# Moving products of the first chunk's feed-forward layer in between its last adapters

## Chip, cores and metric

The kernel runs on one core of one Trainium2 chip. The metric is the device time of one execution in microseconds (us); lower is better. All data are float32.

## The reference, cut to what matters

`x` holds 32 batches of 64 rows (tokens here) by 1024 columns. Four residual layers follow each other:

```python
x = x + ssm_convolution(x)                      # FFT convolution, masked by length
x = x + einsum('bsi,boi->bso', x, W1[id1])      # one 1024x1024 weight per batch
x = x + einsum('bij,bkj->bik', x, W2[id2])      # another one per batch
gate = x @ W_gate.T + 0.5 * (x @ A_gate[id].T) @ B_gate[id].T    # 2752 hidden rows
up   = x @ W_up.T   + 0.5 * (x @ A_up[id].T)   @ B_up[id].T
act  = silu(gate) * up
x = x + act @ W_down.T + 0.5 * (act @ A_down[id].T) @ B_down[id].T
```

The two middle layers are called adapters below: each batch picks one of 16 weights for each of them. The last layer is the gated feed-forward layer with a low-rank term of rank 16 per batch.

## The kernel before, in words

The 32 batches are cut in four chunks of eight, so a chunk has 512 token columns (`TC`); x lies with its 1024 features on 128 partitions in eight k tiles. The convolution of all chunks comes first. Then the 16 adapters of chunk 0 run (eight batches, two layers; batch b's second layer comes after batch b+1's first). Then `ffn` (L902) runs for each chunk, and the adapters of the next chunk are slipped into its matmuls.

An adapter (L297) takes eight weight tiles of 512 KB, each in 16 matmuls' worth of records on TensorE (PE); then VectorE (DVE) transposes the result and adds it to x. Weight tiles come over SyncE's (SP's) DMA queue into `wpool`, nine rotating buffers (`ROTATING`). Some tiles of the first adapters were fetched during the convolution into memory of their own (`early`, `late`), which is used up before the twelfth adapter.

In the gated layer 2688 of the 2752 hidden rows are computed by a Strassen-Winograd scheme with seven products for eight: in chunk 0 on halves of the tokens (256 columns, `TH`) and of the features (`halves`, L526), later on quarters (`quarters`, L624). The last 192 rows, the plain ones, are `rest` (L781), ordinary products with three weight tiles `wr`. The scheme needs sums of weights (`stationary`, `sides`, L481 to L488) and sums of x (`moving`, L495; `moving_of`, L848), all on DVE. In chunk 0 `halves` also makes the sums of a second level for the later chunks: `kept` (L534) writes a block of sums into one of two buffers, and a DMA on GpSimd's (POOL's) queue stores it (L548). A third and a fourth block of the same call (L603, L608) wait for the stores of the first two.

A call of `halves` has two column blocks m = 0, 1, and in each the products 0, 5, 6, 4, 1, 2, 3 in that order, four matmuls of 256 columns each. Product 1 adds onto product 0's bank, 2 onto that of 5 and 4, 3 onto that of 6; DVE adds and ScalarE (ACT) copies the results out between them. `gated` (L745) makes two calls, gate and up. After the first pair of blocks `ffn` runs `rest` and then the down products (L1063), whose terms for the plain rows need `rest1`.

The low-rank products (`low_rank`, L420) multiply x by columns of 32 for each pair of batches: four pairs, each into its own 32 partitions of one bank.

PE's order is that of the program throughout (manual schedule, L129). DVE's and ACT's is so from L349 on, that is once the memory of the first phase is given back (`first.close()`, L347); the other queues are ordered by the framework's scheduler. Between the adapters stand, before the change, only products of the first plain weight tile: the first 256 tokens behind the twelfth adapter (`LEFT_AT`), and then, behind the last one, the next 128 (L331).

Of the kernel before, what the change touches and what calls it, by code (L numbers as in the profile page):

```python
# [19 lines left out]
P = 128  # L20
# [12 lines left out]
MG = 2  # L33
NG = FM // MG
EARLY = 16
LEFT_AT = 11
LATE = 7
FIRST_LOADS = 8
MORE_LOADS = 3
# [37 lines left out]
def kernel(  # L77
# [38 lines left out]
    def ps_tile(name):  # L116
        return psum.tile([P, 512], F32, tag="ps", name=name)
# [200 lines left out]
    def adapters(c):  # L318
        for layer, b in layers(c):
            yield adapter(layer, b)  # L320

    def left_tile():
        wt = wpool.tile([P, KT, P], F32, tag="w", name="wr0_0")
        nc.sync.dma_start(wt.rearrange("p k f -> p (k f)"), wr[0])
        return wt, ps_tile("pr0_0")

    def left_part(wt, ps, t0, t1):

        tokens = slice(t0, t1)
        for kt in range(KT):  # L330
            nc.tensor.matmul(  # L331
                ps[:, tokens],
                wt[:, kt, :],
                xs[0][:, kt, tokens],
                start=(kt == 0),
                stop=(kt == KT - 1),
            )


    for i, _ in enumerate(adapters(0)):  # L340
        if i == LEFT_AT:
            left0 = left_tile()
            left_part(*left0, 0, TH)

    left_part(*left0, TH, TH + TQ)
    done_first = [loads[-1]]
    first.close()  # L347

    ctx.enter_context(tc.manual_schedule(engines={DVE, ACT}))  # L349
# [67 lines left out]
    def pair(j):  # L417
        return slice(2 * R * j, 2 * R * (j + 1))

    def low_rank(at, n, x_of, name):  # L420


        ps = ps_tile(f"pl_{name}")[:, : 2 * H]
        for i in range(n):
            x_i = x_of(i)
            for j in range(BC // 2):
                nc.tensor.matmul(  # L427
                    ps[pair(j)],
                    at[:, i, pair(j)],
                    x_i[:, 2 * H * j : 2 * H * (j + 1)],  # L430
                    start=(i == 0),
                    stop=(i == n - 1),
                )
        return ps
# [72 lines left out]
    def low_rank_of(c, gi, g):  # L507
        name = f"{c}_{gi}_{g}"
        lt, copy = expand(b_rows(c, 2 * gi + g), name, [("gu"[g], i) for i in range(4)])
        return lt.rearrange("p (i m) t -> p i m t", i=2), copy  # L510

    def halves_sides(gi, g, m):

        name = f"{gi}_{g}_{m}"
        wt = []
        for i in (0, 1):
            pool, tag, bufs = (wpool, "w", ROTATING) if i or m else (gpool, "wx", 1)
            t = pool.tile([P, 2, KH, P], F32, tag=tag, name=f"wf{i}_{name}", bufs=bufs)
            nc.sync.dma_start(
                t.rearrange("p k s f -> p (k s f)"), (wg, wu)[g][i, MG * gi + m]  # L520
            )
            wt.append(t)
        st = qpool[0].tile([P, 3, KH, P], F32, tag=f"s{m}", name=f"s_{name}")
        return wt, st, stationary(wt, KH, st)

    def halves(c, gi, g, o, xb, sides0, early, also=lambda: None):  # L526

        name = f"{c}_{gi}_{g}"
        lt, copy_lt = low_rank_of(c, gi, g)
        wts, sts, sides_of = ([x] for x in sides0)  # L530

        kept_first = []
# [35 lines left out]
        for m in range(MG):  # L568
            ws = sides_of[m]

            def product(ps, j, start):
                for kt in range(KH):
                    nc.tensor.matmul(  # L573
                        ps,
                        ws[j][:, kt, :],
                        xb[j][:, kt, :],
                        start=start and kt == 0,
                        stop=kt == KH - 1,
                        skip_group_check=True,
                    )  # L580


            pa, pb, pc = (ps_tile(f"pf{i}_{name}_{m}")[:, :TH] for i in range(3))
            c11, c12, c21, c22 = (
                o[:, i, m, t * TH : (t + 1) * TH] for i in (0, 1) for t in (0, 1)
            )
            u, v = (
                gpool.tile([P, 2 * TQ], F32, tag=f"u{i}", name=f"u{i}_{name}_{m}", bufs=1)
                for i in range(2)
            )  # L590
            product(pa, 0, True)
            nc.scalar.copy(u, pa)
            product(pb, 5, True)
            nc.scalar.copy(v, pb)
            nc.vector.tensor_add(u, v, u)
            if m == 0:
                copy_lt()
                for at_, x in zip((wts, sts, sides_of), halves_sides(gi, g, 1)):
                    at_.append(x)
                also()  # L600
            else:
                kept_parts()
                kept(2)  # L603
            product(pc, 6, True)
            nc.vector.tensor_add(c22, pc, u)
            product(pb, 4, True)
            nc.vector.tensor_add(c22, pb, c22)  # L607
            kept(3 * m)  # L608
            product(pa, 1, False)
            nc.scalar.copy(c11, pa)  # L610
            product(pb, 2, False)
            nc.vector.tensor_add(c12, pb, u)
            if m == 0:
                kept(1)
            else:
                early()
            product(pc, 3, False)
            nc.vector.tensor_add(c21, pc, u)
            o_m = o[:, :, m]
            nc.vector.tensor_add(o_m, o_m, lt[:, :, m])  # L620
# [3 lines left out]
    def quarters(c, gi, g, o, xb, _, early, also=lambda: None):  # L624
# [117 lines left out]
        (p3,) = unit((2,), lambda: None)  # L742
        add(c12, c12, p3)

    def gated(c, gi, xb, sides0, between, early):  # L745

        f = quarters if c else halves
        act = apool.tile([P, 2, MG, TC], F32, tag="act", name=f"act_{c}_{gi}")  # L750
        sides0 = f(c, gi, 0, act, xb, sides0, lambda: fill(1.3 if c else 2.6))
        between(2 * gi)

# [27 lines left out]
    def rest(c):  # L781


        wts, pss = [], []

        def load():
            i = len(wts)
            wt = wpool.tile([P, KT, P], F32, tag="w", name=f"wr{i}_{c}")
            into = wt.rearrange("p k f -> p (k f)")
            last_wr[:] = [nc.sync.dma_start(into, wr[i]).ins]  # L790
            wts.append(wt)

        def products():
            i = len(pss)
            ps = ps_tile(f"pr{i}_{c}")
            for kt in range(KT):
                nc.tensor.matmul(  # L797
                    ps,
                    wts[i][:, kt, :],
                    xs[c][:, kt, :],  # L800
                    start=(kt == 0),
                    stop=(kt == KT - 1),
                )
            pss.append(ps)

        if c == 0:
            left_part(*left0, TH + TQ, TC)
            wts.append(left0[0])
            pss.append(left0[1])
            nc.scalar.copy(rest1, pss[0])  # L810
            yield
        else:
            load()
        bt = b_rows(c, 2 * NG)
        load()
        yield
        if c:
            products()
            nc.scalar.copy(rest1, pss[0])
        yield  # L820
        products()
        lt, copy = expand(bt, f"{c}_rest", (("g", 0), ("u", 1), ("u", 2), ("g", 2)))
        copy()
        nc.vector.tensor_add(lt[:, 0], lt[:, 0], rest1)
        nc.vector.tensor_add(lt[:, 1], pss[1], lt[:, 1])
        nc.scalar.activation(rest1, lt[:, 0], AF.Silu)
        nc.vector.tensor_mul(rest1, rest1, lt[:, 1])
        load()
        products()
        v, up = lt[:, 2], lt[:, 3]  # L830
        nc.vector.tensor_add(v, pss[2], v)
        nc.scalar.copy(up[SECOND], v[FIRST])
        a = rest2.rearrange("p i t -> p (i t)")
        nc.gpsimd.memset(a[FIRST], 0.0)
        nc.scalar.activation(a[SECOND], v[SECOND], AF.Silu)
        nc.vector.tensor_mul(a[SECOND], a[SECOND], up[SECOND])
        yield
# [7 lines left out]
        ps = low_rank(at, KT, lambda i: x_c[:, i, :], f"{name}_{c}")  # L845
        nc.vector.tensor_mul(tms[name], ps, bmask)

    def moving_of(c):  # L848

        x_c = xs[c]  # L850
        xq = [
            x_c[:, k * KH : (k + 1) * KH, t * TH : (t + 1) * TH]
            for k in (0, 1)
            for t in (0, 1)
        ]

        if c == 0:
            xd = qpool[0].tile([P, 7, KH, TH], F32, tag="xd", name=f"xd_{c}")
            for i, q in enumerate((0, 2, 3)):
                nc.scalar.copy(xd[:, 4 + i], xq[q])  # L860
            xb = moving(*xq, *(xd[:, i] for i in range(4)))
            return (xd[:, 4], xd[:, 5], xd[:, 6], *xb[3:])


        xd = qpool[0].tile([P, 7, 7, KQ, TQ], F32, tag="xd", name=f"xd_{c}")

# [251 lines left out]
        return steps[0] if more_come else None  # L1118

    tables = [columns(ag, 0, KT, "g_0"), columns(au, 0, KT, "u_0", ("cu", "lt"))]  # L1120
    ats = [in_order() for in_order in tables]
    xb = moving_of(0)
    for name, at in zip("gu", ats):
        prepare(0, name, at)
    sides0 = halves_sides(0, 0, 0)
    for c in range(NCK):
        xb = ffn(c, xb, sides0, adapters(c + 1) if c + 1 < NCK else iter(()))
        sides0 = None
# [490 lines left out]
```

## Time and profile before

| what | value |
|---|---|
| median of 3 runs (lowest, highest) | 2311.53 us (2307.45, 2314.43) |
| profiled execution, its span | 2313.8 us |
| PE busy, share | 2249.8 us, 97% |
| PE weight loads | 1868.0 us, 81% |
| DVE | 1320.6 us, 57% |
| ACT | 380.0 us, 16% |
| POOL | 270.6 us, 12% |
| mean granted PE clock | 0.998 |
| DMA | 684.96 MB, 296 GB/s |
| twelfth adapter of chunk 0 ends | 286.87 us |
| sixteenth adapter of chunk 0 ends | 329.83 us |
| first product of the first gated call | 338.68 us |
| second gated call's first product | 364.40 us |
| first product of the later `rest` | 393.13 us |
| down products begin | 408.17 us |

The profile is one execution, 2.3 us longer than the median. Times in it count from its first instruction. A matmul in float32 shows as two records, and the shown end of the last record of a group lies a little behind the start of the next group, because matmuls are pipelined; the pace is read from starts. L numbers are lines of the kernel before. In a timeline row the brackets give how long the engine was idle before the row and what it waited for.

### The profile page before, as it was taken

To read this page: it belongs to the slowest core of one execution; us is meant where nothing else is said; L and a number is where in the kernel's file an instruction comes from. 1 tells how busy PE (TensorE), PEld (TensorE's weight loads), DVE (VectorE), ACT (ScalarE), POOL (GpSimd) and SP (SyncE) were. 2 spreads that over 40 slices of the span, in tenths; PEclk is the share of its full clock that TensorE was granted. 3 is DMA by queue.
4 is the path that set the end of the run, shared out by engine and by line. 5 is a ranking of instruction groups with operands and counts; after the bars stand their busy time and mean duration, and the time that the engine had idled before them with its cause. 6 is when DMAs were issued, how large, how long until landed. Compare 5 with 4: busy or idle time off the path is not lost.

```text
span 2313.8 us, 53743 instructions
## 1 busy us (share of the span) xinstructions
PE 2249.8 (97%) x21706; PEld 1868.0 (81%) x21706; DVE 1320.6 (57%) x2791; ACT 380.0 (16%) x822; POOL 270.6 (12%) x388
## 2 busy tenths in 40 slices
PE   5999989999999999999999999999999999999999
PEld 4996557787777789688778889688769889799998
DVE  7511127567446776546535676646535676477585
ACT  4300001011001112111102212121102212121220
POOL 3423003111101121000000011000000011100000
PEclk9999999999999999999999999999999999999999
DMA  8999997879997957879997957879997947285582
GB/s 306 354 370 394 407 403 280 317 289 354 365 343 293 350 174 258 304 285 360 350 357 279 358 167 265 297 292 358 355 351 288 363 152 276 87 298 203 191 280 68
DMA packets 201802, 684.96 MB, mean 296 GB/s; under 512 B 26178, under 2 KB 28482, under 8 KB 201042
## 3 DMA queue, kind: packets, MB, share of 16 engines
q1 hardware_dynamic: 169714, 590.77, 69.5%
q0 software_dynamic: 25184, 82.37, 9.6%
q10 hardware_dynamic: 6656, 8.39, 1.0%
q8 instruction: 171, 2.80, 0.5%
q14 instruction: 77, 0.63, 0.1%
HBM read 614.02 MB, written 67.40 MB: 295 GB/s over the span
## 4 chain that ended last, share of the span: by engine, by line
PE 78%; DMA 14%; issue 5%; DVE 2%; POOL 1%; POOLq 0%; SPq 0%; ACT 0%; DVEq 0%
PE pq L664 28%; PE po L1063 22%; PE pa L304 11%; DMA wa<-in_w 7%; PE pc L1404 5%; PE pf L573 5%; PE pr L797 3%; DMA wa<-sums 2%; DMA sums<-kept 1%; PE pe L456 1%; DMA hk<-kp 1%; PE pl_d L427 1%; DMA kp<-ks 1%; DMA wf<-in_wg 0%; DMA wr<-in_wr 0%
## 5 line engine op out<-in xcount | busy, mean ns | idle before, releaser
L304 PE MATMUL pa<-wa,x 128*32 128x256 f32 x7760 | 449.1, 381 | 19.3 <-DMA wa<-in_w 16.8
L664 PE MATMUL pq<-xd,wa 128*128 128x128 f32 x3360 | 415.9, 275 | 1.3 <-DMA wa<-sums 0.9
L304 PEld LDWEIGHTS pa<-wa,x 128*32 128x32 f32 x7760 | 241.8, 110 | 209.9 <-DMA wa<-in_w 49.1
L664 PEld LDWEIGHTS pq<-xd,wa 128*128 128x128 f32 x3360 | 395.0, 192 | 2.3 <-DMA wa<-sums 2.2
L664 PE MATMUL pq<-xd,wb 128*128 128x128 f32 x2520 | 324.1, 276 | 0.6 <-DVE x L316 0.4
L664 PEld LDWEIGHTS pq<-xd,wb 128*128 128x128 f32 x2520 | 300.7, 192 | 4.7 <-DVE x L316 0.6
L314 DVE STREAM_TRANSPOSE y<-pa 128x512 f32<-128x512 f32 x64 | 45.9, 717 | 286.6 <-PE pa L304 286.6
L1063 PE MATMUL po<-act,wd 128*128 128x256 f32 x640 | 168.6, 386 | 0.0
L1404 PE MATMUL pc<-uf,hk 128*128 128x256 f32 (+7 forms) x1024 | 153.3, 312 | 12.2 <-DMA hk<-kp 9.5
L1063 PE MATMUL po<-actd,s 128*128 128x256 f32 x640 | 164.2, 379 | 0.0
L1063 PE MATMUL po<-actd,wd 128*128 128x256 f32 x640 | 164.2, 379 | 0.0
L1404 PEld LDWEIGHTS pc<-uf,hk 128*128 128x128 f32 x1024 | 148.4, 195 | 16.6 <-issue 7.9
L355 POOL DMA_INDIRECT bgu<-in_bgu,rows x44 | 51.4, 1168 | 924.0 <-PE pe L456 827.2
L573 PE MATMUL pf<-xd,wf 128*128 128x256 f32 x640 | 150.9, 381 | 0.0
L1063 PEld LDWEIGHTS po<-act,wd 128*128 128x128 f32 x640 | 117.8, 190 | 29.9 <-issue 14.6
L482 DVE TENSOR_TENSOR s<-wd 128x256 f32<-128x256 f32 x80 | 33.8, 423 | 184.1 <-PE po L1063 184.0
L573 PEld LDWEIGHTS pf<-xd,wf 128*128 128x128 f32 x640 | 121.2, 191 | 17.4
L1063 PEld LDWEIGHTS po<-actd,s 128*128 128x128 f32 x640 | 121.6, 190 | 16.5
L1063 PEld LDWEIGHTS po<-actd,wd 128*128 128x128 f32 x640 | 121.6, 190 | 16.5
L1095 ACT COPY uo<-po 128x256 f32<-128x256 f32 x48 | 17.9, 373 | 622.3 <-PE po L1063 620.2
L573 PE MATMUL pf<-xd,s 128*128 128x256 f32 x480 | 115.9, 385 | 3.9 <-DVE up L607 2.7
L573 PEld LDWEIGHTS pf<-xd,s 128*128 128x128 f32 x480 | 91.0, 191 | 20.0 <-DVE up L607 4.4
(235 smaller groups left out, 2566.4 us busy)
## 6 DMA issues: line engine op xcount, KB each, us to landing
wa<-in_w SPq DMA_DIRECT2D x485, 512.0 KB, 7.0
wa<-sums SPq DMA_DIRECT2D x210, 512.0 KB, 5.8
wb<-parts SPq DMA_DIRECT2D x120, 384.0 KB, 5.3
wd<-in_wd SPq DMA_DIRECT2D x80, 512.0 KB, 7.0
wb<-in_wq SPq DMA_DIRECT2D x90, 384.0 KB, 5.9
hk<-kp SPq DMA_DIRECT2D x30, 1024.0 KB, 8.8
sums<-kept POOLq DMA_DIRECT2D x30, 1024.0 KB, 7.2
wf<-in_wg SPq DMA_DIRECT2D x20, 512.0 KB, 7.1
```

The costliest lines, as they stand in the source:

```text
L304: nc.tensor.matmul(acc[i * S : (i + 1) * S, s * 256 : (s + 1) * 256], xs[c][:, kt, lo + s * S : lo + (s + 1) * S], wt[:, i * 256 : (i + 1) ...
L314: nc.vector.transpose(y, acc)
L355: nc.gpsimd.indirect_dma_start(out=t, out_offset=None, in_=table, in_offset=bass.IndirectOffsetOnAxis(ap=at_, axis=0),)
L427: nc.tensor.matmul(ps[pair(j)], at[:, i, pair(j)], x_i[:, 2 * H * j : 2 * H * (j + 1)], start=(i == 0), stop=(i == n - 1),)
L456: nc.tensor.matmul(ps[:, at_ * 2 * H : (at_ + 1) * 2 * H], bt[pair(j), g], tms[table][pair(j)], start=(g == 0), stop=True, skip_group_chec ...
L482: nc.vector.tensor_add(s1, a21, a22)
L573: nc.tensor.matmul(ps, ws[j][:, kt, :], xb[j][:, kt, :], start=start and kt == 0, stop=kt == KH - 1, skip_group_check=True,)
L664: nc.tensor.matmul(ps[:, to * TQ : (to + 1) * TQ], w[i][:, k, :], xb[:, j, SLOT[i], k, :], start=start and k == 0 and to == 0, stop=k == K ...
L797: nc.tensor.matmul(ps, wts[i][:, kt, :], xs[c][:, kt, :], start=(kt == 0), stop=(kt == KT - 1),)
L1063: nc.tensor.matmul(pss[j], *term, start=(s0 == m0 and i == 0 and home[j] % 2 == 0), stop=(end and i == len(terms) - 1 and not late), skip_ ...
L1095: nc.scalar.copy(u1, p1)
L1404: nc.tensor.matmul(ps[:, j, d * B :], hk[:, j, d * P : (d + 1) * P], uf[:, i + j, : KT - d, :].rearrange("p k b -> p (k b)"), start=(d == ...
```

## The change

- The memory of the first phase is given back behind the twelfth adapter instead of the sixteenth (`OWN_ENDS`), so that buffers of the gated layer exist from there on; DVE's and ACT's program order begins there too.
- Between the last adapters now stand: the first 256 tokens of all three plain weight tiles (`begin_rest`; only the first tile is kept, the other two are loaded again for the second half in `rest`), products 0 and 1 of both column blocks of the first gated call (`begin_products`), and the low-rank products of gate and up for batch pairs 0 and 1 (`begin_low_rank`). Those of pairs 2 and 3 stay behind the last adapter.
- The four weight tiles of the first gated call are loaded into places of their own (`weight_places`: one buffer of before and the memory of activation tiles that are not in use yet), not into `wpool`: two ahead of the thirteenth adapter, two behind the last one.
- x's sums are made by batches (`part`): batches 4 and 5, then 6, then 7, each as soon as x has them.
- `halves` leaves out products 0 and 1 where they were begun and takes their stored results; `rest` computes only tokens 256 to 511 in chunk 0, and its sums come in two instructions each.

The core of the diff:

```diff
-LEFT_AT = 11
+OWN_ENDS = 12
...
-    for i, _ in enumerate(adapters(0)):
-        if i == LEFT_AT:
-            left0 = left_tile()
-            left_part(*left0, 0, TH)
-
-    left_part(*left0, TH, TH + TQ)
-    done_first = [loads[-1]]
+    layers0 = adapters(0)
+    for _ in range(OWN_ENDS):
+        next(layers0)
     first.close()
...
-            product(pa, 0, True)
-            nc.scalar.copy(u, pa)
+            if begun:
+                p1 = p1s[:, m]
+            else:
+                product(pa, 0, True)
+                nc.scalar.copy(u, pa)
+                p1 = u
             product(pb, 5, True)
             nc.scalar.copy(v, pb)
-            nc.vector.tensor_add(u, v, u)
+            nc.vector.tensor_add(u, v, p1)
...
-            product(pa, 1, False)
-            nc.scalar.copy(c11, pa)
+            if not begun:
+                product(pa, 1, False)
+                nc.scalar.copy(c11, pa)
...
+        def add_to(o, ps, a, begun):
+            nc.vector.tensor_add(o[:, t0:], ps[:, t0:], a[:, t0:])
+            if t0:
+                nc.vector.tensor_add(o[:, :t0], begun, a[:, :t0])
...
+    def begin_rest(i):
+        wt, ps = rest_tile(i, "first")[0], ps_tile(f"pr{i}_first")
+        rest_part(0, wt, ps, 0, TH)
+        nc.scalar.copy((rest1, rest2[:, 0], rest2[:, 1])[i][:, :TH], ps[:, :TH])
+        return wt
...
+        def part(b0, b1):
+            t = slice(b0 * H, b1 * H)
+            nc.scalar.copy(xd[:, 6, :, t], xq[3][:, :, t])
+            moving(*(q[:, :, t] for q in xq), *(xd[:, i, :, t] for i in range(4)))
...
+    wr0 = begin_rest(0)
+    for m in range(MG):
+        first_weight(m, 0)
+    xb, part = first_moving()
+    next(layers0)
+    part(0, 2)
+    begin_rest(1)
+    next(layers0)
+    begin_rest(2)
+    begin_products(0)
     ats = [in_order() for in_order in tables]
-    xb = moving_of(0)
-    for name, at in zip("gu", ats):
-        prepare(0, name, at)
-    sides0 = halves_sides(0, 0, 0)
+    next(layers0)
+    part(2, 3)
+    begin_products(1)
+    for name in "gu":
+        begin_low_rank(name, early_pairs)
+    next(layers0)
+    done_first = [loads[-1]]
+    for m in range(MG):
+        first_weight(m, 1)
+    left0 = wr0, ps_tile("pr0_0")
+    rest_part(0, *left0, TH, TH + TQ)
+    part(3, 4)
+    for name in "gu":
+        begin_low_rank(name, late_pairs)
+    nc.vector.tensor_mul(tms["g"], low["g"], bmask)
+    sides0 = (*halves_sums(0, 0, 0, wfs[0]), wfs[1])
+    nc.vector.tensor_mul(tms["u"], low["u"], bmask)
```

`rest_tile` loads one plain weight tile, `rest_part` does its eight matmuls for some tokens, `next(layers0)` runs one adapter, `first_weight(m, i)` loads one gated weight tile, and `begin_products(j)` does product j of both column blocks.

## The prediction

> **What bounds the kernel now.** I read the page for the shares (TensorE, PE, is busy 97% of 2313.8 us), then the chain of waits, which lies in loads of adapter weights up to 330 us, then windows and timeline of both sides of that point. Windows of 20 us (columns: length; busy us and count of PE, PEld, DVE, ACT, POOL; granted clock; DMA share; GB/s):
>
> ```profile
> 300.00:320.00 20.00, 16.82 (x256) 6.68 (x248) 2.60 (x4) 0.00 (x0) 0.00 (x0) 1.00 1.03 408
> ...
> 340.00:360.00 20.00, 20.00 (x94) 17.29 (x93) 14.42 (x25) 4.12 (x11) 4.72 (x7) 1.00 0.82 314
> ```
>
> Between the last adapters the DMA is full and PE has holes; 20 us after them PE is full and DVE busy for 72%. The holes, in the timeline:
>
> ```profile
> 287.13 3.69 PE L331 MATMUL pr<-x,wr 128*128 128x256 f32 x16 [0.31 <-DMA wr<-in_wr]
> ...
> 290.75 7.52 PE L304 MATMUL pa<-wa,x 128*32 128x256 f32 x128
> ...
> 316.35 1.07 PE L304 MATMUL pa<-wa,x 128*32 128x256 f32 x16 [0.19 <-DMA wa<-in_w]
> 317.64 1.07 PE L304 MATMUL pa<-wa,x 128*32 128x256 f32 x16 [0.22 <-DMA wa<-in_w]
> ```
>
> One 512 KB tile lands each 1.28 us, and an adapter is eight of them. With its tiles there, PE does an adapter in 7.1 us (the 128 records that start at 417.37 take 7.09), 0.88 a tile. From the end of the twelfth adapter (286.87) to that of the last (329.83) are 42.96 us with 3.6 + 4 x 7.1 = 32.0 us of work: 11.0 us of holes, all that can be filled there.
>
> **The moved work, piece by piece.** A 128x256 product of four matmuls (eight records) takes PE 1.73 us (starts at 340.51 and 342.23 in the timeline), so eight matmuls of the plain rows (rest) take 3.46, 3.6 with the change of shape (287.13 to 290.75). Added in the holes: two such halves of the rest, 7.2; four products, 6.9; and the low-rank products of the early batch pairs. Those last need care:
>
> ```profile
> 329.76 2.05 PE L331 MATMUL pr<-x,wr 128*128 128x128 f32 x16
> ...
> 331.75 1.96 PE L427 MATMUL pl_g<-x,at_g 128*32 128x128 f32 x64
> ```
>
> Sixteen full-width records of 128 columns take as long as 64 records of 32 rows: the four pairs run side by side in four column groups, eight steps of 0.22 us. No row shows two pairs alone. From below, half the work is half the time: 0.9 a table. [...] I take 1.75, since the row already shows eight steps at the full-width pace. So the early half adds 3.5 us (g and u), and the late half behind the last adapter still takes 3.5, as all of it does now. By the other figure the sum would be 3.5 less.
>
> **The loads.** From 240 to 340 us the DMA moves 405 to 420 GB/s and is full, so a transfer put in front of an adapter delays it by its own 1.28 us. New ahead of the last adapter are rest weights 1 and 2 (they are loaded again later, so they are extra) and two gated weights: 4 x 1.28 = 5.1 us. The other two gated weights come behind the last adapter's tiles, as now. Destinations: the early tiles they overlap were read by 267 us, so I expect SP not to be held. The adapter-table copies on ACT come after the products now, so the next tables and a row gather on POOL move from 216-225 to about 321-331; POOL is idle from 228 to 338, and the gather lands (6.4 us) ten us before its use. The memset of rest2 moves behind the rest's sums on POOL, 0.5 us beside ACT's 1.3. All nothing on the path; if POOL were late, expand would wait for it directly.
>
> **Until the first gated product.** Rest 0 ends at 290.75. Adapter 13's tiles follow two gated weights: the last lands at 287.1 + 10 x 1.28 = 299.9, done 300.8 (3 us of hole stay). Rest weight 1 lands at 301.2: rest to 304.8. Adapter 14 is held by its last tile, 311.4, done 312.3. Rest weight 2 at 312.7: to 316.3. First products to 319.8, adapter 15 to 326.9, second products 330.4, low rank 333.9, adapter 16 to 341.0. Before it was 329.8. Behind it 2.0 + 3.5 + 2.0 + 1.3 = 8.8 us up to the first gated product left, as now (329.83 to 338.68). x's sums by batches cut DVE's work behind the last adapter from 4 x 1.22 to 4 x 0.42, but PE does not wait there now, so 0. **+11.2 us.**
>
> **The first gated call.** Four products leave it, 6.9 us of PE. But the call also makes sums that DVE writes and POOL stores, in two buffers:
>
> ```profile
> 349.49 0.74 POOL L548 DMA_DIRECT2D sums<-kept  x1 [7.99 <-DVE kept L485]
> ...
> 356.11 0.69 DVE L482 TENSOR_TENSOR kept<-s 128x512 f32<-128x512 f32 x1 [0.70 <-DMA sums<-kept]
> ...
> 359.64 1.59 PEld L573 LDWEIGHTS pf<-xd,s 128*128 128x128 f32 x8 [0.38 <-DVE act L607]
> ```
>
> The first kept block stands behind product 4; its store takes 6.6 us, the third block waits for it (356.11), and the two adds that PE's next product needs stand behind the third block in DVE's order. PE waits 0.38 us already. Only one product ahead of that chain goes, so the chain moves up by 1.7 us; the other 5.2 become a wait: I expect PE idle for about 1 us at column block 0 and 4.5 before product 2 of block 1. **-1.7 us.**
>
> **The rest later.** Its two 512-column products (393.13 to 400.09, 401.20 to 408.17) halve: 7.0 us of PE less. Its sums stand behind 7.8 us of adds to the next chunk's x on DVE:
>
> ```profile
> 400.33 7.81 DVE L264 TENSOR_TENSOR x<-x,cv 128x512 f32<-128x512 f32 x8
> ...
> 409.45 0.69 DVE L827 TENSOR_TENSOR rest<-rest,lt_rest 128x512 f32<-128x512 f32 x1
> ...
> 411.62 0.59 PE L1063 MATMUL po<-rest,wm 128*128 128x256 f32 x2
> ```
>
> DVE is without a pause from 391.3 to 410.1, and PE takes `rest` at 411.62, 1.5 us later. PE would now ask 7.0 us sooner and DVE is 0.2 to 0.4 later (each split add is two instructions of 0.42 for one of 0.69). So PE waits about 5.9 us. **-1.0 us.**
>
> **The clock.** Two new waits of over 4 us. In windows of 1 us after the 1.99 us wait at 386-388:
>
> ```profile
> 389.00:390.00 1.00, 1.00 (x4) 0.81 (x3) 0.66 (x2) 0.00 (x0) 0.04 (x1) 0.50 0.96 389
> 390.00:391.00 1.00, 1.00 (x4) 0.81 (x3) 0.00 (x0) 0.00 (x0) 0.52 (x1) 0.50 1.04 414
> ```
>
> The granted clock is half for 3.4 us, and the first product takes 3.40 us where 1.89 is usual: 1.5 us. [...] From 0 (the slow stretch falls into the wait) to 1.7 each; I take 1.5, the row. **+3.0 us.**
>
> Sum against the profiled execution: 11.2 - 1.7 - 1.0 + 3.0 = +11.5, a span of 2325.3 for 2313.8. That span is 2.3 above the median of 2311.5, so the median goes to 2323.0. From 416 us on PE is busy to over 98% and the shift stays to the end.
>
> **Rivals.** A measurement of this kernel can tell about 0.3% (6.9 us) from no change. The forecast, waits on DVE in both places and a half-empty hole in adapter 13, has 0.60: +8 to +15.
> *Holes better filled, clock kept, 0.22.* SP's order is made by a scheduler; if it puts the gated weights behind adapter 13's tiles, 2.6 us of its hole go, and the slow clock may fall into the waits: 11.2 - 2.6 - 1.7 - 1.0 = +5.9, 2317.4. For it: the pieces are small. Against it: SP's queue kept program order for the rest weight at 276.84.
> *PE stays the bound behind the adapters, 0.12, the other side.* Place: the third kept block and `rest`. If the kept stores land in 3 us or so and DVE runs the rest's sums ahead of x's adds, the 13.9 us of removed products count in full: 11.2 - 13.9 = -2.7, 2308.8. It decides by the length of the two waits with their clock: 11.2 of waits and 3.0 of clock are expected; under 2.7 together the kernel is not slower at all. For it: one store in the trace took 5.0 us. Against it: the median is 7.2, and DVE's order is the program's.
> *The early loads hold SP, 0.06.* If a destination is not free at 277, SP's queue stops before adapter 13's tiles and the pipe of eight tiles runs dry: up to 10 us on top, 2333.
>
> **The numbers.** Slower by over 0.3%: the forecast, the last rival and a fifth of the first, 0.71. Within: 0.27. Faster by over 0.3%: 0.02, the third with the old 2 us wait gone too. The range leaves out most of the third rival and the last: 2313 to 2330.
>
> **What would show it.** The last adapter ends near 341 us; the early low-rank parts take 1.75 us per table; PE idle for about 4.5 us behind the kept block and 6 us before the first `rest` term; two more half-clock stretches. Wrong if those waits are absent, if two pairs take half the time, or if adapter 13 runs without a hole.

## The result, and the profile after

| | before | after |
|---|---|---|
| median (lowest, highest), 7 runs each on one chip | 2311.74 us (2307.45, 2314.43) | 2320.82 us (2317.69, 2325.44) |
| profiled execution, its span | 2313.8 us | 2321.7 us |
| mean granted PE clock | 0.998 | 0.997 |

The kernel after takes 1.0036 of the time before (95% interval 1.0022 to 1.0051), which is 5.1 to 11.8 us more; the medians differ by 9.1 us. The forecast was 2323.0 us, 11.5 more. The two windows that were shown of before, in the profile after (same columns):

```profile
300.00:320.00 20.00, 19.52 (x212) 13.57 (x214) 4.75 (x8) 3.55 (x7) 0.10 (x1) 1.00 0.98 381
340.00:360.00 20.00, 19.14 (x175) 16.94 (x174) 14.70 (x29) 3.34 (x8) 3.13 (x5) 1.00 0.89 347
```

PE now works 19.5 us of the 20 among the last adapters, where it worked 16.8. From 300 us on the holes are filled. How far the path is longer, the timeline tells (PE only):

```profile
285.52 3.69 PE L331 MATMUL pr_first<-x,wr_first 128*128 128x256 f32 x16 [0.30 <-DMA wr_first<-in_wr]
...
314.53 1.89 PE L1170 MATMUL pf_first<-x,wf_first 128*128 128x256 f32 x8
...
328.77 1.94 PE L423 MATMUL pl_g<-x,at_g 128*32 128x128 f32 x32
...
339.30 2.05 PE L331 MATMUL pr<-x,wr_first 128*128 128x128 f32 x16
341.28 1.94 PE L423 MATMUL pl_g<-x,at_g 128*32 128x128 f32 x32
343.05 1.92 PE L423 MATMUL pl_u<-x,at_u 128*32 128x128 f32 x32
```

The last adapter ends where the row at 339.30 begins, 53.78 us behind the first `rest` tile (285.52). In the kernel before it was 42.63 us (287.13 to 329.76). Two batch pairs of the low rank take 1.77 us (341.28 to 343.05), as four did before (331.75 to 333.52). Further on, the two waits (the rows of POOL, DVE and PE that make them up, in order of time):

```profile
357.06 0.74 POOL L549 DMA_DIRECT2D sums<-kept  x1 [7.61 <-DVE kept L481]
363.48 0.69 DVE L478 TENSOR_TENSOR kept<-s 128x512 f32<-128x512 f32 x1 [1.85 <-DMA sums<-kept]
366.54 0.43 DVE L614 TENSOR_TENSOR act<-pf,act 128x256 f32<-128x256 f32 x1
367.02 3.44 PE L574 MATMUL pf<-xd,s 128*128 128x256 f32 x8 [3.83 <-DVE act L614]
...
406.36 7.69 DVE L264 TENSOR_TENSOR x<-x,cv 128x512 f32<-128x512 f32 x8
415.42 0.69 DVE L836 TENSOR_TENSOR rest<-rest,lt_rest 128x512 f32<-128x512 f32 x1
416.17 1.22 PE L1080 MATMUL po<-rest,wm 128*128 128x256 f32 x2 [5.95 <-DVE rest L836]
417.18 1.91 PE L1080 MATMUL po<-act,wd 128*128 128x256 f32 x4
```

A store of `kept` takes 6.4 us (357.06 to 363.48), DVE's third kept block waits for it, and the add at 366.54 that PE needs stands behind that block; PE waits 3.83 us. At 416.17 PE waits 5.95 us for `rest`, behind the eight adds to chunk 1's x. Behind both the granted clock is 0.50, for 3.4 us from 367.41 and for 6.8 from 415.20: the first product takes 3.44 us where 1.89 is usual, and at 417.18 four records take 1.91 where 1.03 is usual.

Since the same work begins 1 to 3 us sooner or later in each execution, all positions from here on count from the start of the first `rest` tile's products. "Before again" is a second trace of the unchanged kernel, told of below.

| stage, us | before | before again | after |
|---|---|---|---|
| to the first gated product | 51.55 | 51.50 | 62.46 |
| first gated call | 25.72 | 25.68 | 25.48 |
| second gated call | 28.73 | 25.56 | 24.93 |
| rest and down products of the first block, up to the down low-rank products | 22.90 | 23.38 | 25.17 |
| sum: the low-rank products of the first down block start at | 128.90 | 126.12 | 138.04 |

Chunk 0 has three blocks of down products. The sums end at the first of them, so "chunk 0 shorter" in the expectations below means the stretch up to there. The low-rank products near 322 us, which one of them calls chunk 1's, are those of chunk 0's second block (609.08 in the first trace of before, whose chunk 1 has its own first low-rank products at 847 us). The waits "in chunk 1" lie between the low-rank products of the first and the second block, where chunk 1's adapters run.

### The profile page after: what moved, and what is told of

Same layout as the page of the kernel before. It is cut to its first block, busy times and chain, and to the rows that moved or that the text cites. A ratio compares the mean times of both kernels' runs of the same rounds, so it can differ in the third digit from the quotient of the medians.

```text
span 2321.7 us, 53818 instructions
## 1 busy us (share of the span) xinstructions
PE 2251.8 (97%) x21738; PEld 1880.9 (81%) x21738; DVE 1320.7 (57%) x2801; ACT 380.8 (16%) x827; POOL 264.2 (11%) x388
## 4 chain that ended last, share of the span: by engine, by line
PE 82%; DMA 12%; DVE 3%; issue 2%; POOL 0%; SPq 0%; ACT 0%; POOLq 0%; DVEq 0%
PE pq L672 28%; PE po L1080 23%; PE pa L304 12%; PE pf L574 7%; DMA wa<-in_w 6%; PE pc L1496 5%; PE pr L331 3%; DMA hk<-kp 2%; PE pe L452 2%; DMA sums<-kept 1%; DMA wr_first<-in_wr 1%; PE pl_d L423 1%; PE pr_first L331 0%; DMA actd_first<-in_wg 0%; DMA wa<-sums 0%
## 5 line engine op out<-in xcount | busy, mean ns | idle before, releaser
L1496 PE MATMUL pc<-uf,hk 128*128 128x256 f32 (+7 forms) x1024 | 153.1, 311 | 11.2 <-DMA hk<-kp 10.4
L350 POOL DMA_INDIRECT bgu<-in_bgu,rows x44 | 44.6, 1013 | 923.1 <-PE pe L452 831.2
L1080 PEld LDWEIGHTS po<-actd,wd 128*128 128x128 f32 x640 | 122.2, 191 | 16.8
L574 PE MATMUL pf<-xd,wf 128*128 128x256 f32 x576 | 135.5, 381 | 0.0
L574 PEld LDWEIGHTS pf<-xd,wf 128*128 128x128 f32 x576 | 108.7, 190 | 15.5
```

Source lines behind the costliest of these rows:

```text
L350: nc.gpsimd.indirect_dma_start(out=t, out_offset=None, in_=table, in_offset=bass.IndirectOffsetOnAxis(ap=at_, axis=0),)
L574: nc.tensor.matmul(ps, ws[j][:, kt, :], xb[j][:, kt, :], start=start and kt == 0, stop=kt == KH - 1, skip_group_check=True,)
L1080: nc.tensor.matmul(pss[j], *term, start=(s0 == m0 and i == 0 and home[j] % 2 == 0), stop=(end and i == len(terms) - 1 and not late), skip_ ...
L1496: nc.tensor.matmul(ps[:, j, d * B :], hk[:, j, d * P : (d + 1) * P], uf[:, i + j, : KT - d, :].rearrange("p k b -> p (k b)"), start=(d == ...
```

## The experiments

Each ratio is to the kernel before on the same chip, with its 95% interval; on these chips that kernel's medians were 2312.0 to 2313.9 us. Diffs are cut to the core (`...`), and to the kernel after where nothing else is said. Waits and times inside a run come from its one profiled execution.

**The low-rank products whole, behind the last adapter.**

```diff
     begin_products(1)
-    for name in "gu":
-        begin_low_rank(name, early_pairs)
...
-        begin_low_rank(name, late_pairs)
+        begin_low_rank(name, range(BC // 2))
```

> The changed kernel, with the low-rank products of all four batch pairs behind the last adapter, none between the adapters. Theory (two pairs side by side take as long as four): 3.5 us of TensorE work leave the stretch before the last adapter and nothing is added behind it, so the first gated product comes 3.5 us sooner and the time is about 2317.3 for 2320.8. Rival (half the pairs, half the time): 1.8 us move from before the last adapter to behind it, and the time stays at 2320.8.

Measured: 1.0031 (1.0019 to 1.0043), which can't be told from after. The stage to the first gated product is 2.9 us shorter, PE's wait in the first gated call 4.75 us instead of 3.83, and the down low-rank products stand at 134.2 instead of 138.0. So the early half does cost about what the row of four pairs said (by the rival the stage would have kept its length), and part of what is saved comes back as a longer wait for the kept store, which took 7.4 us here.

**The adds to chunk 1's x by GpSimd.**

```diff
-                    nc.vector.tensor_add(xv, xv, t.rearrange("p i k -> p k i")[:, rows_])
+                    eng = nc.gpsimd if c == 1 else nc.vector
+                    eng.tensor_tensor(
+                        xv, xv, t.rearrange("p i k -> p k i")[:, rows_], ALU.add
+                    )
...
+                if c == 1:
+                    with tc.issue_after(last_kept[0]):
+                        add()
```

> The changed kernel, with the eight adds to the second chunk's x made by GpSimd behind its last store of the first gated pair, instead of by VectorE ahead of the plain rows' sums. Theory (those adds are what holds the plain rows' sums): TensorE's wait of 5.95 us before the first down product with the plain rows goes, and the half clock behind it (3.0 us) with it: about 2312 for 2320.8, less up to 2 us if GpSimd's adds are late for the next adapter. Rival (the sums are late for another reason, the products or ScalarE): the wait stays at 5 us or more and the time within 2 us of 2320.8.

Measured: 1.0054 (1.0041 to 1.0067), no faster than the kernel after: both expectations missed. DVE and POOL in the timeline:

```profile
398.67 12.18 DVE L486 TENSOR_TENSOR s<-s,wd 128x256 f32<-128x256 f32 x1
398.81 11.75 POOL L265 TENSOR_TENSOR x<-x,cv 128x512 f32<-128x512 f32 x8
```

An add that takes DVE 0.42 us in after (398.36 there) stood for 12.18 us, as long as GpSimd's eight adds of 1.5 us each. PE then waited 6.72 us, with 10.2 us of half clock. The work went to another engine and the wait stayed. The run says nothing about the order of DVE's queue, which is what it was for.

**The third kept block behind the two adds** (only where products were begun).

```diff
                 kept_parts()
-                kept(2)
+                if not begun:
+                    kept(2)
...
+            if m and begun:
+                kept(2)
             kept(3 * m)
```

> The changed kernel; in the first gated call the third block of second-level sums is made behind the two adds that TensorE's product 2 needs, not ahead of them. Theory (the block waits for its buffer's store and holds the adds behind it): TensorE's wait of 3.83 us and the half clock behind it (1.9 us) go, of which up to 2 us come back as a wait for the next weights' sums on VectorE: 2315.5 to 2317.5. Rival (TensorE waits because VectorE as a whole has too much work in this call): the wait moves to the next call in full, and the time is within 1 us of 2320.8.

Measured: 1.0013 (1.0004 to 1.0023). DVE in the timeline:

```profile
363.00 0.42 DVE L615 TENSOR_TENSOR act<-pf,act 128x256 f32<-128x256 f32 x1 [1.08 <-PE pf L574]
363.56 0.69 DVE L478 TENSOR_TENSOR kept<-s 128x512 f32<-128x512 f32 x1
```

The add now stands ahead of the block and waits for PE alone. The 3.83 us wait and its half clock are gone, and the first gated call takes 20.48 us instead of 25.48. The second takes 25.45 instead of 24.93, so the wait did not move there, as the rival had it. That the wait came from the place of one DVE block, and that it cost this call 5.0 us, is shown.

**The first two gated weights behind the third plain tile.**

```diff
     wr0 = begin_rest(0)
-    for m in range(MG):
-        first_weight(m, 0)
...
     begin_rest(2)
+    for m in range(MG):
+        first_weight(m, 0)
     begin_products(0)
```

> The changed kernel, with the first two gated weight tiles loaded directly ahead of their use, behind the fourteenth adapter and the third plain tile, instead of ahead of the thirteenth adapter. Theory (the DMA is full, so what stands first makes the hole): the thirteenth adapter ends 2.6 us sooner, the last adapter about 2.5 us sooner, and the time is about 2318.3. Rival (TensorE's work alone sets the last adapter's end): no change, 2320.8. A third: the products wait for these tiles instead, up to 1 us.

Measured: 1.0046 (1.0031 to 1.0060), no better than after: a miss for the theory's time. The last adapter ended 2.4 us sooner, as the theory had it, but the kept store took 8.8 us (353.90 to 362.73) instead of 6.4, and PE waited 6.24 us in the first gated call instead of 3.83.

**The rest's halves put back.**

```diff
-    begin_rest(1)
-    next(layers0)
-    begin_rest(2)
+    next(layers0)
...
-        t0 = 0 if c else TH
+        t0 = 0
```

> The kernel after, with the plain rows' first halves of tiles 1 and 2 put back behind the second gated call; the four products, the early low-rank products and the sums by batches stay. Theory (the holes are too small for what was put there, so the halved rest terms cost the stage about as much as they save later): the last adapter ends about 5 to 6 us later than in the kernel before, not 11.2; the rest is as long as before, without the 5.95 us wait of TensorE in front of it and the half clock behind that wait; 7 to 8 us below the kernel after, about 2313. Rival (the halves of the rest are worth their 7 us at the end, whatever they displace): 1.5 us above the kernel after, about 2322.

Measured: 1.0038 (1.0025 to 1.0052), level with after: a miss for the theory, and not the rival's reason either. The stage was 5.0 us shorter and the 5.95 us wait at the rest was gone, both as the theory had them. But (POOL and DVE, then PE, in the timeline):

```profile
350.72 0.74 POOL L549 DMA_DIRECT2D sums<-kept  x1 [7.60 <-DVE kept L481]
353.58 0.74 POOL L549 DMA_DIRECT2D sums<-kept  x1 [2.12 <-DVE kept L481]
360.54 0.69 DVE L478 TENSOR_TENSOR kept<-s 128x512 f32<-128x512 f32 x1 [5.26 <-DMA sums<-kept]
...
364.08 2.50 PE L574 MATMUL pf<-xd,s 128*128 128x256 f32 x5 [7.24 <-DVE act L614]
```

and in windows of 1 us inside that wait:

```profile
357.00:358.00 1.00, 0.00 (x0) 0.00 (x0) 0.00 (x0) 0.00 (x0) 0.00 (x0) 1.00 1.04 430
358.00:359.00 1.00, 0.00 (x0) 0.00 (x0) 0.00 (x0) 0.00 (x0) 0.00 (x0) 1.00 1.02 410
359.00:360.00 1.00, 0.00 (x0) 0.00 (x0) 0.00 (x0) 0.00 (x0) 0.00 (x0) 1.00 1.02 410
```

The store took 9.8 us (350.72 to 360.54); no engine works, and the DMA is full. The first gated call took 30.25 us instead of 25.48, with 10.2 us of half clock. So 4.8 of the 5 us came back at the first wait behind the stage.

**The loads that are added to chunk 1's x behind the third kept store**, in the kernel with the rest's halves put back (their rows read `cv<-cd`, four of 512 KB):

```diff
-            with tc.issue_after(done_first[0]):
+            with tc.issue_after(all_kept[2] if c == 1 else done_first[0]):
                 nc.sync.dma_start(
                     t.rearrange("p i k -> p (i k)"),
```

> The kernel with the rest's halves put back, with one more edit: the four 512 KB loads that are added to chunk 1's x are issued behind the third kept store of the first call instead of beside the first. Theory (the gain of the shorter stage was lost because the first kept store then shared the DMA with a weight load and the last of these four loads, and took 9.8 us instead of 6.4): the store takes 6 to 7 us, TensorE's wait in the first gated call is 3.5 to 4.5 us instead of 7.24, with 3.4 to 6.8 us of half clock instead of 10.2; 4 to 6 us below that kernel, about 1.0015 of the kernel before. Rival (the store is held by the weight load that column block 1 needs, or by its own packets): it takes over 9 us as before, and nothing is gained, 1.004.

Measured: 1.0028 (1.0013 to 1.0042). SyncE issued three of the four loads at 332.16 and the last at 351.63, within 0.3 us of where they were without the edit, counted from the first `rest` tile: the edit did not move them, and the run is a repeat of the one above. The store took 9.9 us again, the wait 7.28. Which transfer holds the store is therefore open. The traces have only a row of cases, not an experiment. With the fourth of these loads issued within 1 us of the store it took 8.8, 9.8 and 9.9 us (the weights later, and the two kernels with the rest's halves back). Without it, it took 6.4 us in after, 7.4 with the low rank whole, and 6.6 in before.

**The rest's sums ahead of the adds to x.**

```diff
             if block == 0:
                 next(left)
...
-                flush()
+                if c:
+                    flush()
...
+            if c == 0 and block == 0:
+                flush()
+                down_sides()
```

> The kernel after, with VectorE making the rest's sums ahead of the eight adds to chunk 1's x; those adds and the next sums stand behind. Theory (VectorE's total work in this stretch sets the end, so the wait only moves): the 5.95 us wait of TensorE at the rest goes, and one of 4 to 5 us comes in front of chunk 1's first adapter; 1 to 4 us below the kernel after, 2317 to 2320. Rival (only the order of VectorE's queue costs it): wait and half clock both go, 5.95 and 3.0 us, about 8.9 below the kernel after, 2312.

Measured: 1.0024 (1.0014 to 1.0034), some 3 us below after by the ratios, the theory's size. The 5.95 us wait was gone, and PE reached the first down low-rank products at 129.1 (138.0 in after), so VectorE's order was its cause. In chunk 1's first adapter it then waited 1.98 us for x and 1.8 for adapter weights, and ran 3.4 us at half clock:

```profile
418.15 5.78 PE L304 MATMUL pa<-wa,x 128*32 128x256 f32 x72 [1.98 <-DVE x L264]
```

**Both waits attacked at once**, the third kept block and the rest's sums:

> The kernel after with both waits attacked: the third kept block behind the two adds (it took 4.9 us away alone), and the rest's sums ahead of the adds to chunk 1's x (2 to 4 us alone). Theory (the two waits are separate terms of the sum, and each edit takes its own): both gains add up to 7 to 9 us, level with the kernel before, 1.000 with an interval of 0.001. Rival (chunk 1's adapter weights come no sooner, the DMA being full there in every kernel, so what is gained before them is lost in front of them): no more than the better of the two alone, 1.0015 to 1.002, and over 3 us of TensorE's time in waits for adapter weights in chunk 1.

Measured: 1.0011 (1.0000 to 1.0022), between the two: the ratio alone separates neither. The rival's sign is there, 5.7 us of waits for adapter weights up to the second block's low-rank products (1.7 in after). PE in chunk 1's first adapter, and SyncE's waits from 395 to 426 us (us in total, times, longest), the last line from before:

```profile
411.75 0.61 PE L304 MATMUL pa<-wa,x 128*32 128x256 f32 x8
413.75 4.09 PE L304 MATMUL pa<-wa,x 128*32 128x256 f32 x72 [1.38 <-DVE x L264]
419.84 1.07 PE L304 MATMUL pa<-wa,x 128*32 128x256 f32 x16 [2.00 <-DMA wa<-in_w]
```

```profile
SPq L170 <- DVE x L264: 8.1, 3, 5.8
SPq L170 <- PE pr L331: 5.4, 2, 2.9
```

```profile
SPq L170 <- DVE x L264: 5.4, 4, 1.4
```

The stretch up to the first down low-rank products was 13.2 us shorter than in after, and at those of the second block 6.2 us of that were left. The rival's reason, a full DMA, is not seen: from 400 to 420 us its share is 0.70. The loads of chunk 1's adapter weights (L170) wait 8.1 us for the adds to x, one of them 5.8 us (in before 5.4 in all, none over 1.4), since their buffers hold what is being added. So an add that is put back delays x and the next weights alike; that this is the whole of the loss is not shown.

**The kernel before, with the second block's down table loaded behind the last kept store.**

```diff
...
+            if c == 0 and loaded[0] == 1:
+                pass
+            elif loaded[0] < len(BLOCKS):
                 raw.append(down_table(loaded[0]))
...
+                if c == 0:
+                    with tc.issue_after(last_kept[0]):
+                        raw.append(down_table(1))
```

> The kernel before, with one edit: the second block's down table is loaded behind the last kept store of the pair. Theory (in the kernel before GpSimd's first kept store of the second gated call is issued 1.8 us after its sums because the eight table loads stand ahead of it in the queue; the change only moved them out of the way): the store is issued within 0.4 us of its sums, the 1.99 us wait at 385.9 to 387.9 and the half clock behind it vanish, 3 to 4 us below the kernel before, about 2308. Rival (the late issue has another cause): no change, 2311.7.

Measured: 1.0001 (0.9993 to 1.0009), no change in the whole, as the rival had it. The store was issued 0.3 us after its sums, where it was 1.8 in before's first trace, so the table's loads did delay it. The 1.99 us wait turned into 1.17 and 1.02 in two places, without half clock, and the first block's low-rank products came 1.4 us sooner; the whole was not shorter.

**The kernel before, with the third kept block later in all calls** (the edit above, without its condition).

> The kernel before, with the third kept block made behind the two adds in all four calls and nothing else. Theory (the 1.99 us wait at 385.9 and the half clock behind it are this block's price, and the change got rid of them by shifting the second call against the stores): wait and half clock gone, chunk 0 shorter by 3.5 us and the whole by 2 to 4, 0.9985. Rival (chunk 1's adapter weights give it back): chunk 0 shorter by 3.5 but the whole within 1 us, 1.000.

Measured: 1.0013 (1.0002 to 1.0025), slightly slower: a miss for both. The profiled execution had no wait over 1 us in the second call and reached the first block's low-rank products 2.6 us sooner than before's first trace, but then had 5.4 us of waits for adapter weights up to the second block's.

**The kernel before again.**

> The kernel before, unchanged, to see how far one profiled execution differs from another behind chunk 0. If TensorE's waits for adapter weights in chunk 1 come and go by themselves, they differ here by over 2 us from the 1.1 us of the first trace; if they follow from the kernel, they are again 1 us, and the start of chunk 1's down low-rank products lies 322 us behind the start of the first rest tile's, within 0.7 us.

A span of 2306.8 us, 7.0 less than the first trace of the same program; 3.0 of them lie ahead of the first `rest` tile, 2.8 in the stages of the table. Its second gated call, POOL and PE:

```profile
373.61 0.74 POOL L548 DMA_DIRECT2D sums<-kept  x1 [2.31 <-DVE kept L482]
...
383.31 1.99 PE L573 MATMUL pf<-xd,s 128*128 128x256 f32 x8 [0.54 <-DVE up L607]
```

The 1.99 us wait of the first trace, from which the forecast took its price of half clock, is 0.54 here and has no half clock behind it: the store was issued 1.3 us behind its sums, not 1.8, and took 6.2 us, not 7.1. The waits for adapter weights up to the second block's low-rank products are 1.3 us, not 1.1, within the bound that was set; those products stand 2.4 us sooner than in the first trace, outside it. So neither answer holds as it was put: the stages up to the second call repeat within 0.1 us, the second call differs by some 3 us between these two executions, and `rest` by 0.5.

**Of the change only the four products** and the sums by batches, with the third kept block later in all calls:

> Of the change only the four products between the last adapters and the sums by batches; the rest's halves and the low-rank products are where they were before, and the third kept block is made behind the two adds in all calls. Theory (the products are the one moved part that fits the holes; its kept wait goes with the third block's place): against the kernel before the stage to the first gated product is 2.5 us longer, the first gated call 5.2 shorter, the second 3.3 shorter; about 2305.7. Rival (the first call's wait comes back because the stores then land no sooner, as with the low-rank products whole): 3 to 5 us more, 2309 to 2311.

Measured: 0.9992 (0.9982 to 1.0002), 4.9 us below the kernel after with its third block later by the ratios; the forecast, 0.997 as a ratio, is missed. The rival's size is met, but without the wait that was its reason. The stage was 4.5 us longer than before, not 2.5; the first gated call 5.2 shorter, as expected; the second 25.78 us, near before's own 25.56 in its second trace. PE then waited 7.6 us for adapter weights up to the second block's low-rank products (1.1 in before). The version can't be told from the kernel before, and no version here beats that measurably.

## Why the prediction was right, and what it missed

**The direction, and the mechanism, held**: work that was put into 11 us of holes filled them and pushed the last adapter back, and what was taken away later (6.9 and 7.0 us) came back, most of it as waits on DVE (3.83, 0.86 and 5.95 us), the rest as half clock. That the total comes so near is in part luck: of the four stages two fit, and the misses of the other two, -3.8 and +1.8 us, are of opposite sign.

**Until the first gated product**, forecast +11.2 us: +10.9. The last adapter was forecast for 341.0 on the clock of before's trace; it ended at 287.13 + 53.78 = 340.9. The value chosen for two batch pairs (1.75 us a table) was 1.77; the other end, 0.9, would have put the stage 3.5 us too short. Taking the early half away gave back 2.9. Neither the rival of better filled holes nor that of a held SyncE came true: it issued the two gated weights at 276.47 and 277.75 and adapter 13's tiles from 279.13 on, so it was not held, and the adapter took from 289.35 to 299.3, with the hole of about 3 us that was forecast.

**The first gated call**, -1.7 and 1.5 for the clock, -0.2 in all: -0.2. The wait at product 2 of block 1 was 3.83 us for 4.5, the one at block 0 0.86 for 1. Moving one DVE block took 5.0 us out of this call, so its place, ahead of the adds and behind a store, was the cause.

**The rest later**, -1.0 and 1.5 for the clock: +2.3 against the first trace, +1.8 against the second. The wait was 5.95 us for 5.9. The term that was mis-sized is **the clock**: 6.8 us of half clock from 415.2 to 422.0, not 3.4. From the first `rest` term to the down low-rank products are 7.39 us (416.17 to 423.56) where before has 4.41 (411.62 to 416.03), so 3.0 us of work were lost and not 1.5. With -6.8 for the halved products, +5.95 and +3.0 the sum is +2.1.

Why two pieces of half clock and not one, the windows show. The half-clock stretches of after start at 70.46, 367.41 and 415.20 us, which is 87 and 14 times 3.413 us apart, and those of before at 70.88 and 388.31, 93 times; so the time of these traces can be cut into cells of that length. After, then the run with the weights later, in such cells around the wait for `rest` (columns as above, the second is PE's busy time):

```profile
411.78:415.20 3.42, 0.00 (x0) 0.00 (x0) 3.42 (x6) 0.52 (x1) 0.00 (x0) 1.00 0.65 198
415.20:418.61 3.41, 2.44 (x6) 1.99 (x7) 1.99 (x5) 1.73 (x4) 0.52 (x1) 0.50 0.97 311
418.61:422.02 3.41, 3.41 (x10) 2.69 (x9) 2.30 (x6) 0.00 (x0) 0.00 (x0) 0.50 0.23 94
```

```profile
411.38:414.79 3.41, 0.00 (x0) 0.00 (x0) 3.31 (x6) 0.63 (x1) 0.00 (x0) 1.00 0.94 296
414.79:418.20 3.41, 3.10 (x7) 2.52 (x8) 2.03 (x5) 1.62 (x3) 0.52 (x1) 0.50 0.68 258
418.20:421.62 3.42, 3.42 (x34) 2.77 (x36) 2.48 (x7) 0.00 (x0) 0.00 (x0) 1.00 0.24 74
```

In both an idle cell is followed by one at half clock. In after PE is idle for the first 0.97 us of that one too, and the next is at half clock as well; in the other run it is idle for 0.31 us, and the next is at full clock. The waits were 5.95 and 5.29 us. So these two waits cost two cells and one, as they fell on the cells, and the cells need not lie alike in two executions: counted from the first `rest` tile, one begins at 101.18 us in before, and in after the nearest at 102.37. The forecast's one price of 1.5 us had no room for that.

**The second gated call** stood at 0 in the forecast and shows -3.8. At most 0.6 of that is shown to be the change's: the second trace of before has 25.56 us there, 3.2 less than the first, without the wait. Two traces don't tell how often before has it, so whether the change makes it rarer is open. Against the second trace the stages sum to +11.9, against the first to +9.1. The forecast treated a wait of one execution as a fixture of the kernel.

**The rival of the other side** said that with both waits away the 13.9 us of removed products would count in full, 2.7 us below before, and that under 2.7 us of waits and clock the kernel is not slower. Both waits were taken away. The first down low-rank products then came 4.1 us before those of the first trace and 1.3 before those of the second, so up to there the rival's sum is about right. It fails in the sentence that from 416 us on the shift stays to the end. That holds for the kernel after (+9.1 and +9.7 at the low-rank products of the first two blocks, against the first trace, and +9.5 at the end), but with both waits gone 7.1 of the 13.2 us gained on it were lost again up to the second block. The eight adds have to be made somewhere, and chunk 1's first adapter and its weights both wait for them. That is not all of it: with the adds in their old place the products alone (7.6 us) and before with its third block later (5.4 us) also wait long for adapter weights, while before again, which is there just as early, waits 1.3. What sets these waits is open.

**What was moved, part by part**: the products are level with before once their kept wait is gone. The halves of the rest and the early low-rank products come on top of that with 4.9 us (0.9992 against 1.0013; each ratio is good to 0.001, so some 3 us either way, and the two versions differ also in where the third block stands in the other three calls). That the halves cost the stage 5.0 us is shown by putting them back; in that run 4.8 us came back at the kept store.

## To carry to other kernels

Put into a hole no more than its length: what is over pushes the whole chain back, and the work that it saves later is worth only what the other engines' queues let PE use. Before pricing a cut in one stage, look at the first wait for a store or load behind it: cuts of 2.4 and 5.0 us were eaten there, and a third of one of 2.9. Price the half clock behind a wait as a range, not as one figure: here none came behind a wait of 2.00 us, and 10.2 us behind one of 7.24. Take a second trace of the kernel before, for a wait of 2 us in one execution can be absent in the next.

## What the runs showed of the hardware that was not expected

- With the adds to chunk 1's x on GpSimd, a VectorE add that takes 0.42 us elsewhere took 12.18. It began 0.14 us ahead of GpSimd's eight adds (398.67 and 398.81), which stood back to back for 11.75 us, 1.47 to 1.53 each, and it ended 0.29 us behind the last of them. So it stood for the length of all eight and not of one alone; what held it no run shows.
- The length of a wait did not tell how much half clock followed: 6.8 us behind a wait of 7.28, 10.2 behind one of 7.24, 3.4 behind one of 1.99, none behind one of 2.00. In before and after each stretch lasted one cell (3.413 us) or two (6.827). There PE's idle time within a cell goes with it, from 33 us on, where the clock records begin, to 2310 us: the five cells at full clock that a half-clock cell followed had 1.99, 2.90, 3.02, 3.39 and 3.41 us of it, and no other cell at full clock had over 1.57. At half clock the one cell with 0.97 us of idle time was followed by another, the five with none by full clock. What lies between these values the two traces do not show.
- The first kept store of the first gated call, the same work in every kernel, took between 6.4 and 9.9 us from its issue to the release of its buffer.
